# Holding back the second expert's gathers and the weight sums, and making queries and keys for four sequences at a time, in a two-layer transformer kernel

## The chip, the cores and the metric

The kernel runs on one core of a Trainium2 chip. The metric is the device time of one execution in microseconds (us), lower is better. Several executions of the kernel before are shown by their median; one further execution was recorded by the hardware profiler, and every view below comes from that one. All data is float32 except for a few small one-hot products.

## The reference

The input x has 32 sequences of 128 tokens of 512 numbers. Two layers follow one another.

```python
# layer 0
h   = layernorm(x) + silu(cond) @ W_ada.T
q, k, v = 16 heads of 64 of h @ Wqkv.T;  q, k normed per head
x   = x + softmax(q k.T / 8) v @ Wout.T
tok = x.reshape(4096, 512)
gate = softmax(tok @ Wgate.T)                 # 8 experts
vals, idx = top_k(gate.T, 512)                # each expert picks 512 tokens
g   = layernorm(tok[idx])
y   = gelu_tanh(g @ fc1[e].T) @ fc2[e].T * vals
tok = tok.at[idx].add(y)
# layer 1
n   = adaln1(x, cond);  q, k, v = n @ wq.T + bq, n @ wk.T + bk, n @ wv.T + bv   # 16 heads of 32
x   = x + softmax(q k.T / sqrt(32)) v @ wo.T + bo
x   = x + gelu(adaln2(x, cond) @ w1.T + b1) @ w2.T + b2
```

## The kernel before

**The schedule.** All work is written as operations handed to a scheduler of the kernel's own (`Sched.op`): the engine or engines that may do it, an estimated duration, what it reads (`r`) and writes (`w`), and a priority. When the kernel is built, `Sched.run` plays a clock over these and fixes one order of instructions for each engine; buffers of SBUF and banks of PSUM are given out in that order too. On the chip each engine follows its order and waits by semaphores. So a change of a dependence or of a priority constant can move many instructions. A buffer made with `stands` is no memory; it only orders operations.

**Products.** Most matrix products are cut into blocks of two by two and made with seven block products instead of eight (Strassen in Winograd's form). This needs sums of blocks: of the operands ahead (VectorE, line L1310, or GpSimd, L1311) and of the results behind. Results gather in three PSUM banks, named X, Y and Z, of which one is read (copied by ScalarE or added by VectorE) between two products into it.

**Weight sums.** The last layer's two MLP matrices are cut twice, so that they need sums of blocks of blocks. These are made once, in 22 steps (`w1_outer`, `w2_outer`, `w1_inner`, `w2_inner`) in the shade of layer 0 and of the experts. A step loads four blocks by one `fetch` (L2549, tiles `w1r`, `w2r`, SyncE's queue), adds them on VectorE or GpSimd (tiles `w1n`, `w2n`), and stores the sums by `put` (L2554).

**From layer 0 to the experts.** The last projections of layer 0 (L1976, added at L1984) are stored as tokens (L1991, `tok` and `acc`). For each of 8 experts four indirect DMAs, issued by GpSimd (L2208), gather 128 chosen tokens each into `xg`. VectorE takes their statistics (L501, L502, L504), two small ScalarE activations and three small VectorE operations make the inverse root (L465 to L473), and L2272 writes the normed tile `xng`. TensorE transposes it (L1283, tile `tpg`), ScalarE or VectorE evicts the transposes into `gT` (L2284, L2282), and the products with the first expert matrix begin (L2322), followed by those with the second (L2386). For expert 0 these are spread: the first two tiles are normed one by one, the other two together. While TensorE has nothing to do it runs a few idle products (`spun`, L1225) and finds the tokens of expert 1 (L2143 to L2170). A copy named `fence` (L2214) waits for the fourth gather of expert 0, and later loads wait behind it. The gathers of expert 1 have priority `pe_ - 1000`, ahead of nearly all else.

**The last layer.** The 32 sequences are 16 groups of two (`group(g)`); two groups make one four (`G`, 8 in all), for which the MLP is made at once (`up`, L3027, then `down`, L3109). A group norms its sequences into `nT`, makes queries and keys by `prod_qk` (L2755): in each of seven products q and k stand side by side in one bank, and each matmul has 128 columns of one block row of the group as its moving operand. Values and the output projection come from `chain_T` (L2799) with 256 moving columns of weights. Then come scores (L2855), exponentials (L2859), sums and weighted values (L2867, L2873), the output projection and the second norm. The MLP products of the four before fill TensorE while a group's norms and exponentials are made. MLP weights stream in as pieces of 256 KB, of which `STREAM` may be under way; `gate = inner_done[-(n):][:1]` lets a chain of seven products begin only when the n-th last one is nearly done.

Of the kernel before, what the change touches and what calls it, by code (L numbers as in the profile page):

```python
# [13 lines left out]
AF = mybir.ActivationFunctionType  # L14
# [5 lines left out]
P = 128  # L20
# [1173 lines left out]
def fast_kernel(ctx: ExitStack, tc: tile.TileContext, x, condT, mask, cols, w_ada, wqkv, wout, wout_p, wout_o, wgate,  # L1194
# [998 lines left out]
    def expert(e, after):  # L2193
# [13 lines left out]
        for h in range(NH):  # L2207
            sch.op(POOL, 1.2, lambda h=h: nc.gpsimd.indirect_dma_start(  # L2208
                out=xg[h].t, out_offset=None, in_=tok[:, :],
                in_offset=bass.IndirectOffsetOnAxis(ap=idx[:, e, h : h + 1], axis=0)),  # L2210
                w=[xg[h]], r=[tok_b, (idx_b, e)], lat=2.5, prio=pe_ - 1000 if e == 1 else pe_, job=job)
# [55 lines left out]
        for h in range(NH):  # L2267
            if e == 0 and h == 2:
                norm0((2, 3), pe_ - 1, [xn])
            xn, tp = row(f"xng_{e}_{h}"), bank(f"tpg_{e}_{h}")  # L2270
            mv, y, z = stat[h]
            sch.op(DVE, dve_us(D, 2, True), lambda xn=xn, h=h, mv=mv, y=y, z=z: nc.vector.tensor_scalar(  # L2272
                xn.t, xg[h].t[:, :D], mv.t[:, 2 * z : 2 * z + 1], y.t[:, z : z + 1], ALU.subtract, ALU.mult),
                w=[xn], r=[xg[h], mv, y], prio=px[h], job=job)
# [267 lines left out]

    step_done, room_for, first_steps = [], [(17)], (10)

    def fetch(pieces, pr, job):
# [4 lines left out]
        sch.op(SP, 0.24, f_, w=[b_ for b_, _, _ in pieces], r=[x for _, _, r in pieces for x in r] + step_done[-(2):][:1], lat=4.0, prio=pr,  # L2550
# [64 lines left out]
    for n, step in enumerate(steps):  # L2615
        g = 3 + (3 + n) // 2 - 1
        step_done.append(stands(None))
        if n == first_steps:
            room_for.append((13))
        if n < first_steps:  # L2620
# [3 lines left out]

    for m, (n, s_) in enumerate(at_w):
# [94 lines left out]
    def group(g):  # L2720
        b0 = g * GB
        G, sub = divmod(g, 2)
        pr = LB + G * 1000.0
        pr -= {0: (87), 1: (112), NG4 - 1: (54)}.get(G, 100) - 100
        pn, pat, job = pr - (806) + (12) * sub, pr + (100) + (34) * sub, LJ + G
# [8 lines left out]
        else:  # L2734
            for i in range(GB):
                norm_T([x2[i]], nT, ss1, ss1_b, b0, f"a1_{g}_{i}", pn + i, job, i, True)
                seen_v.append((st.v, 4 + i, 1))


        pp = pn + 8  # L2740
# [49 lines left out]
        def chain_T(n, Bn, rB, Tv, Tn, pr, once, after):  # L2790

            X, Y, Z = (bank(f"{n}{c}_{g}", (P, QD)) for c in "xyz")

            def prod(b_, what, lhs, rr, fresh=True, keep=0):
                w_, wb = l1w[n + what]

                def f_():
                    for k in range(2):
                        nc.tensor.matmul(b_.t, lhs()[:, k, :], w_()[:, k, :], start=fresh and k == 0, stop=True, skip_group_check=True)  # L2799
                sch.op(PE, mm_us(QD, 2), f_, w=[b_], r=rr + [wb], prio=pr, job=job, keep=keep)  # L2800

            prod(X, "11", lambda: Bn(1, 1), [*rB(1, 1), Y, Z], keep=KEEP_A)
            prod(Z, "s1", lambda: Tv(1), [Tn[1]])
            once(1, X)
            prod(Y, "12", lambda: Bn(2, 1), rB(2, 1))
            once(5, Z)
            prod(X, "s2", lambda: Tv(2), [Tn[2]], False)
            after(1, 1, Y)
            once(2, X)
            prod(Z, "s4", lambda: Bn(2, 2), rB(2, 2), False)  # L2810
            prod(X, "s3", lambda: Tv(3), [Tn[3]], False)
            after(1, 2, Z)
            once(3, X)
            prod(X, "22", lambda: Tv(4), [Tn[4]], False)
            after(2, 1, X)

# [18 lines left out]
        chain_T("v", N_, rN, NTv, NTn, pp + 1, once_v, after_v)  # L2835


        x3 = x2
        oTs, both = [], []
        for i in range(GB):  # L2840
# [9 lines left out]
            def quads(scs=scs, i=i):  # L2850
                for t in range(4):
                    for r in range(4):
                        rs = slice(r * 32, r * 32 + 32)
                        qk_ = qk[1 + t // 2, 1 + i].t
                        nc.tensor.matmul(scs[r].t[:, t, :], qk_[rs, 1, t % 2, :], qk_[rs, 0, t % 2, :], start=t == 0, stop=True,  # L2855
                                         skip_group_check=True)
            sch.op(PE, mm_us(S, 5), quads, w=scs, r=[qk[1, 1 + i], qk[2, 1 + i]] + ([gelus[G - 1]] if G else []), prio=pa + 1, job=job)
# [11 lines left out]
            def outs(po=po, pe=pe, i=i):  # L2869
                for t in range(4):  # L2870
                    for r in range(4):
                        h = 4 * t + r
                        nc.tensor.matmul(po.t[r * 32 : r * 32 + 32, t, :], v[i].t[:, h * HD1 : (h + 1) * HD1],  # L2873
# [415 lines left out]
```

## Time and profile before

| | us |
|---|---|
| median of 3 runs | 3107.63 |
| the runs | 3107.51, 3114.08, 3107.63 |
| the profiled execution, its own time | 3113.92 |
| span of its records | 3112.2 |
| TensorE busy | 3074.4 |
| VectorE busy | 2256.6 |
| GpSimd busy | 1284.7 |
| ScalarE busy | 1267.4 |

The span runs from the first to the last record; the profiled execution's own time holds a little more. Windows are given in us from the start of the span: layer 0 lasts to about 1042, the experts to about 1846, the last layer to the end. In a line of the timeline the columns are start and length in us, engine, line of the kernel, operation, output and inputs, shapes and count, and in square brackets the idle time of the engine just before, with what ended it. PE is TensorE, PEld its weight loads, DVE VectorE, ACT ScalarE, POOL GpSimd, SP SyncE. A matmul of float32 leaves two records. The clock is TensorE's granted clock as a share of the full one.

### The profile page before, as it was taken

What the parts mean: (1) busy time and instruction counts of PE and PEld (TensorE: products, weight loads), DVE (VectorE), ACT (ScalarE), POOL (GpSimd) and SP (SyncE); (2) the same over time, 40 slices, a digit from 0 to 9 for tenths busy, and PEclk for the clock granted to TensorE, in tenths of its full rate; (3) what the DMA queues carried; (4) which work ended last, traced back from release to release, by engine and by line L of the source; (5) the groups of instructions that cost most, each with busy time, mean ns of one, the idle gap of its engine ahead of it and who ended that gap; (6) DMA issues with size and microseconds to landing.
All of it is one profiled execution on the core that took longest, in us unless ns stands there. A gap on an engine that the chain in (4) does not pass through costs nothing. (4 is left out here: it accounts for less than half of the span.)

```text
span 3112.2 us, 60678 instructions
## 1 busy us (share of the span) xinstructions
PE 3074.4 (99%) x22656; PEld 2514.9 (81%) x22656; DVE 2256.6 (73%) x4490; ACT 1267.4 (41%) x3241; POOL 1284.7 (41%) x1030
## 2 busy tenths in 40 slices
PE   9999999999999999999999999999999999999998
PEld 5655555555588788888888888999999999999997
DVE  8877888889866688666665446786767676767675
ACT  4455565556500222221222114545463636364543
POOL 2412524434220367765666510334343424243525
PEclk9999999999999999999999999999999999999999
DMA  7556757756585865443333361655555556566576
GB/s 278 190 199 232 240 188 245 265 195 203 186 275 195 278 210 183 112 112 104 111 104 109 99 183 48 197 181 180 187 180 181 184 176 190 170 191 193 170 228 201
DMA packets 350672, 571.97 MB, mean 184 GB/s; under 512 B 33258, under 2 KB 114722, under 8 KB 350114
## 3 DMA queue, kind: packets, MB, share of 16 engines
q1 hardware_dynamic: 341714, 550.38, 54.1%
q0 software_dynamic: 7168, 16.91, 2.8%
q8 instruction: 182, 2.98, 0.4%
q14 instruction: 120, 0.98, 0.1%
q10 hardware_dynamic: 1488, 0.71, 0.1%
HBM read 473.62 MB, written 94.27 MB: 182 GB/s over the span
## 5 line engine op out<-in xcount | busy, mean ns | idle before, releaser
L1311 POOL TENSOR_TENSOR base<-base,base 128x512 f32<-128x512 f32 x335 | 450.6, 1359 | 789.4 <-DVE base L3078 445.9
L3109 PE MATMUL bank<-base,base 128*128 128x128 f32 x3048 | 365.1, 278 | 6.6 <-POOL base L1311 3.5
L3109 PEld LDWEIGHTS bank<-base,base 128*128 128x128 f32 x3048 | 354.2, 193 | 13.8 <-POOL base L1311 3.9
L3027 PE MATMUL bank<-base,base 128*128 128x128 f32 x3048 | 361.6, 275 | 0.5 <-ACT bank L2989 0.2
L3027 PEld LDWEIGHTS bank<-base,base 128*128 128x128 f32 x3048 | 354.3, 192 | 4.6 <-ACT bank L2989 1.2
L1310 DVE TENSOR_TENSOR base<-base,base 128x512 f32<-128x512 f32 (+2 forms) x476 | 307.5, 666 | 35.7 <-ACT base L2971 12.7
L2333 ACT ACTIVATE h<-h,prm 128x256 f32<-128x256 f32 x256 | 114.9, 502 | 255.5 <-DVE h L2327 240.6
L2386 PE MATMUL d<-fc,h 128*128 128x256 f32 x992 | 218.9, 379 | 0.0
L2386 PEld LDWEIGHTS d<-fc,h 128*128 128x128 f32 x992 | 188.0, 190 | 25.3
L3037 ACT ACTIVATE base<-base,prm 128x128 f32<-128x128 f32 x512 | 169.2, 397 | 49.7 <-DVE base L3072 29.2
L2322 PE MATMUL u<-gT,fc 128*128 128x256 f32 x768 | 179.1, 383 | 0.9 <-ACT gT L2284 0.9
L2322 PEld LDWEIGHTS u<-gT,fc 128*128 128x128 f32 x768 | 147.4, 192 | 21.6 <-ACT gT L2284 1.3
L2327 DVE TENSOR_TENSOR h<-v,u 128x512 f32<-128x512 f32 x128 | 86.2, 682 | 65.5 <-PE u L2322 59.5
L2322 PE MATMUL u<-tg,s 128*128 128x256 f32 x512 | 120.9, 379 | 0.0
L2386 PE MATMUL d<-t,hs 128*128 128x256 f32 x512 | 113.4, 379 | 0.0
L2418 POOL DMA_INDIRECT acc<-y,idx x32 | 50.7, 1584 | 149.3 <-DVE y L2411 79.2
L3072 DVE TENSOR_TENSOR base<-bank,base 128x512 f32<-128x512 f32 x96 | 66.0, 688 | 59.5 <-PE bank L3027 54.6
L2322 PEld LDWEIGHTS u<-tg,s 128*128 128x128 f32 x512 | 97.3, 190 | 13.2
L2386 PEld LDWEIGHTS d<-t,hs 128*128 128x128 f32 x512 | 97.2, 190 | 13.2
L3078 DVE TENSOR_TENSOR base<-bank,base 128x512 f32<-128x512 f32 x120 | 82.0, 688 | 30.1 <-PE bank L3027 15.2
L2859 ACT ACTIVATE base<-bank,mbT 128x512 f32<-128x512 f32 x128 | 81.9, 687 | 45.6 <-PE bank L2855 31.5
L2799 PE MATMUL bank<-base,base 128*128 128x256 f32 x384 | 98.1, 382 | 1.3 <-DVE base L2894 0.4
(1880 smaller groups left out, 6858.6 us busy)
## 6 DMA issues: line engine op xcount, KB each, us to landing
base<-w1i SPq DMA_DIRECT2D x224, 256.0 KB
base<-w2i SPq DMA_DIRECT2D x224, 256.0 KB
base<-w2s SPq DMA_DIRECT2D x168, 256.0 KB
fc<-in_fc_dram SPq DMA_DIRECT2D x64, 512.0 KB
fc<-in_fc_dram SPq DMA_DIRECT2D x32, 1024.0 KB
base<-w1s SPq DMA_DIRECT2D x96, 256.0 KB
base<-in_w_dram SPq DMA_DIRECT2D x72, 256.0 KB
otd<-oT SPq DMA_DIRECT2D x56, 256.0 KB
```

Of the source, the lines that this page charges most:

```text
L1310: ways = {DVE: (DVE, dve_us(n), lambda: nc.vector.tensor_tensor(o_(), a_(), b_(), op_)), POOL: (POOL, 0.2 + n / 480, lambda: nc.gpsimd.ten ...
L1311: POOL: (POOL, 0.2 + n / 480, lambda: nc.gpsimd.tensor_tensor(o_(), a_(), b_(), op_))}
L2322: nc.tensor.matmul(ps[n].t[:, t, :], lhs()[:, k, t * P : (t + 1) * P], rhs.t[:, k, :], start=(k == 0), stop=(k == 1))
L2327: sch.op(DVE, dve_us(D), lambda: nc.vector.tensor_tensor(o_.t, a_.t, ps[n].t, ALU.add), w=[o_], r=[a_, ps[n]], prio=pr, job=job)
L2333: sch.op(ACT, act_us(HQ, 1), lambda t=t, c=c: nc.scalar.activation(o_.t[:, t, :], o_.t[:, t, :], AF.Gelu_apprx_tanh, bias=col("b1s", e * 1 ...
L2386: nc.tensor.matmul(ps[n].t[:, j, :], lhs[m].t[:, k, t * P : (t + 1) * P], rhs.t[:, 2 * m + k, :], start=(m == 0 and k == 0), stop=(m == NM ...
L2799: nc.tensor.matmul(b_.t, lhs()[:, k, :], w_()[:, k, :], start=fresh and k == 0, stop=True, skip_group_check=True)
L2859: sch.op(ACT, act_us(D, 1), lambda sc=scs[r], pe=pe[r], b=b: nc.scalar.activation(pe.t, sc.t, AF.Exp, bias=mbT[:, b : b + 1], scale=sm1), ...
L3027: nc.tensor.matmul(b_.t[:, u, :], w_.t[:, u * P : (u + 1) * P], x_(), start=fresh and u == 0, stop=True, skip_group_check=True)
L3037: sch.op(ACT, act_us(S, 1), lambda k=k, u=u, c=c: nc.scalar.activation(o_[k].t[:, u * S : (u + 1) * S], o_[k].t[:, u * S : (u + 1) * S], A ...
L3078: sch.op(DVE, dve_us(D), lambda: nc.vector.tensor_tensor(d_[k].t, flat(src), flat(t_), ALU.add), w=[d_[k]], r=[src, t_], prio=po - 3000, j ...
L3109: nc.tensor.matmul(b_.t, x_()[:, k * S : (k + 1) * S], w_.t[:, k, :], start=fresh and k == 0, stop=True, skip_group_check=True)
```

## The change

Three things change, with a set of constants.

1. The norms of expert 0 write a marker, `ends["normed"]`. The gathers of expert 1 read it, and so do the loads (`fetch`) of the weight-sum steps from number 13 on (`after_norm`). Both are therefore ordered behind all four norms of expert 0.
2. `group` is split into `places`, `norms`, `pair_products` (the old form), `quad_products` and `attend`. The first four keeps the old form for its two groups. For the seven others `quad_products` makes queries and keys of four sequences at once: q and k are two chains of seven products with a bank set each, the moving operand has 256 columns (both sequences of a group), and the two block columns are the two groups. Values are made by `chain_T` with twice as many columns of the bank for the same weights.
3. Constants: priorities in `places`, `up` and `down`, `STREAM` 14 to 13, the gates of `chained` (11 to 0, and `[-0:][:1]` is the first chain of all) and `seeded` (20 to 40).

```diff
-                w=[xg[h]], r=[tok_b, (idx_b, e)], lat=2.5, prio=pe_ - 1000 if e == 1 else pe_, job=job)
+                w=[xg[h]], r=[tok_b, (idx_b, e), *(ends["normed"] if e == 1 else [])], lat=2.5, prio=pe_ - 1000 if e == 1 else pe_, job=job)
...
+            normed = [] if e else [stands(None)]
+            if e == 0:
+                ends["normed"] = normed
...
-                w=[xn], r=[xg[h], mv, y], prio=px[h], job=job)
+                w=[xn, *normed], r=[xg[h], mv, y], prio=px[h], job=job)
...
+    after_norm = [[]]
...
-        sch.op(SP, 0.24, f_, w=[b_ for b_, _, _ in pieces], r=[x for _, _, r in pieces for x in r] + step_done[-(2):][:1], lat=4.0, prio=pr,
+        sch.op(SP, 0.24, f_, w=[b_ for b_, _, _ in pieces], r=[x for _, _, r in pieces for x in r] + step_done[-(2):][:1] + after_norm[-1], lat=4.0, prio=pr,
...
+        if n == 12:
+            after_norm.append(ends["normed"])
...
-        pr -= {0: (87), 1: (112), NG4 - 1: (54)}.get(G, 100) - 100
+        pr -= {0: (90), 1: (112), NG4 - 1: (54)}.get(G, 100) - 100
...
+    def chain_T(n, g, job, Bn, rB, Tv, Tn, pr, once, after, two=False):
+        X, Y, Z = (bank(f"{n}{c}_{g}", (P, 2, QD) if two else (P, QD)) for c in "xyz")
...
+                for m in range(2 if two else 1):
+                    for k in range(2):
+                        nc.tensor.matmul(b_.t[:, m, :] if two else b_.t, lhs()[:, k, m * S : (m + 1) * S], w_()[:, k, :],
+                                         start=fresh and m == k == 0, stop=True, skip_group_check=True)
...
+    def quad_products(G, nTs):
+        pp, job = places(2 * G + 1)[1] + 8, LJ + G
+        N_ = lambda j, l: nTs[l - 1][j - 1].t
...
+        Tn = {n: row(f"n1f{n}_{G}", (P, 2, GT)) for n in (1, 2, 3, 4)}
+        for n, a_, b_ in ((1, nTs[1][0], nTs[0][0]), (2, nTs[1][1], Tn[1]), (3, nTs[1][1], nTs[1][0]), (4, nTs[0][1], Tn[2])):
+            tt(lambda n=n: Tn[n].t, lambda a_=a_: a_.t, lambda b_=b_: b_.t, ALU.subtract, D, [Tn[n]], [a_, b_], pp, job, DVE, False)
+        qk = {}
+        for z in "qk":
...
+            X, Z, Y = (bank(f"{z}{c}_{G}", (P, 2, GT), c == "y") for c in "xzy")
+            t_ = row(f"{z}t_{G}", (P, 2, GT))
...
+                    for u in range(2):
+                        for k in range(2):
+                            nc.tensor.matmul(b_.t[:, u, :], w_()[:, k, u * P : (u + 1) * P], rhs()[:, k, :],
+                                             start=fresh and u == k == 0, stop=True, skip_group_check=True)
...
+            prod(X, "11", lambda: N_(1, 1), rN(1, 1), True, KEEP_A, [Y, Z])
+            prod(Z, "s1", lambda: Tn[1].t, [Tn[1]], True)
+            biased(Y, X, 1, pp - 2)
+            prod(X, "s2", lambda: Tn[2].t, [Tn[2]], False)
+            copied(t_, Z, pp - 1)
+            prod(Y, "12", lambda: N_(2, 1), rN(2, 1), False)
+            biased(Z, X, 1, pp - 2)
+            prod(X, "s3", lambda: Tn[3].t, [Tn[3]], False)
...
+        chain_T("v", f"q{G}", job, N_, rN, lambda n: Tn[n].t, {n: Tn[n] for n in Tn}, pp + 1, once_v, after_v, True)
...
-            pa = pat + (13) * i
+            pa = pat + (16) * i
...
-    STREAM = (14)
+    STREAM = (13)
...
-        gate = inner_done[-(11):][:1]
+        gate = inner_done[-(0):][:1]
...
-        gate = inner_done[-(20):][:1]
+        gate = inner_done[-(40):][:1]
...
-        pr, job = LB + G * 1000.0 + 200 - ({0: (132), NG4 - 2: (135), NG4 - 1: (300)}.get(G, 100) - 100), LJ + G
+        pr, job = LB + G * 1000.0 + 200 - ({0: (132), NG4 - 2: (138), NG4 - 1: (600)}.get(G, 100) - 100), LJ + G
...
-        pr, job = LB + G * 1000.0 + (1137) - ({0: (91), NG4 - 2: (2), NG4 - 1: (1241)}.get(G, 100) - 100), LJ + G
+        pr, job = LB + G * 1000.0 + (1154) - ({0: (0), NG4 - 2: (2), NG4 - 1: (1491)}.get(G, 100) - 100), LJ + G
...
-        form(s1_, a21, a22, ALU.add, pr - (470))
+        form(s1_, a21, a22, ALU.add, pr - (420))
...
-        form(a21, a11, a21, ALU.subtract, pr - (987))
+        form(a21, a11, a21, ALU.subtract, pr - (1037))
...
     for G in range(NG4):
-        got = [group(2 * G + z) for z in range(2)]
+        on = [norms(2 * G + z) for z in range(2)]
+        if G:
+            how = quad_products(G, [nT for _, nT in on])
+        else:
+            how = [pair_products(z, on[z][1]) for z in range(2)]
+        got = [attend(2 * G + z, *on[z], *how[z]) for z in range(2)]
```

## The prediction

> **What bounds the kernel.** I read the share of each engine first, then the windows with the granted clock, then the timeline at the places where TensorE is not full, and the waits of TensorE last.
>
> ```profile
> PE 3074.4 (99%) x22656; PEld 2514.9 (81%) x22656; DVE 2256.6 (73%) x4490; ACT 1267.4 (41%) x3241; POOL 1284.7 (41%) x1030
> ```
>
> TensorE is busy for 3074.4 of 3112.2 us. Only two things can shorten the kernel by much: less TensorE work, or a removed piece of its 38 us of idle time. The windows say where that idle time lies: 7.3 us in 1012:1089 (layer 0 ends, the experts begin), 14.1 us in 2957:3112 (the tail), 3.0 us in 1859:1945 (entry of the last layer), and only 2.7 us in the 1012 us of 1945:2957, the steady part of the last layer. Start of the experts, in 2 us windows (TensorE busy, granted clock, DMA share, GB/s):
>
> ```profile
> 1040.00:1042.00 2.00, 2.00 (x21) 1.00 1.06 416
> 1042.00:1044.00 2.00, 0.74 (x7) 1.00 1.05 413
> 1044.00:1046.00 2.00, 0.00 (x0) 1.00 0.95 327
> 1046.00:1048.00 2.00, 0.00 (x0) 0.67 0.82 248
> ...
> 1054.00:1056.00 2.00, 2.00 (x6) 0.50 1.00 317
> 1056.00:1058.00 2.00, 2.00 (x12) 0.77 1.05 402
> ```
>
> TensorE stops for six microseconds while the DMA engines are full, the clock falls to half at about 1046.7 and comes back at about 1056.9. The timeline of all engines over the same stretch names the chain:
>
> ```profile
> 1035.52 1.46 POOL L2208 DMA_INDIRECT xg<-tok,idx  x1 [3.49 <-DMA acc<-xl]
> ...
> 1042.83 0.69 DVE L501 BATCH_NORM_STATS2 ng_0st<-xg 128x6 f32<-128x512 f32 x1 [0.79 <-DMA xg<-tok,idx]
> ...
> 1046.44 2.15 DVE L2272 TENSOR_SCALAR xng<-xg,ng_0mv,ng_0y 128x512 f32<-128x512 f32 x1
> ...
> 1048.65 2.16 PE L1283 MATMUL tpg<-ident,xng 128*128 128x128 f32 x8 [5.91 <-DVE xng L2272]
> ...
> 1051.71 5.41 PE L2322 MATMUL u<-gT,fc 128*128 128x256 f32 x12 [0.90 <-ACT gT L2284]
> ```
>
> Gather, statistics, norm, transpose, first product. Two links are long for a reason that the change touches. The gather takes 7.31 us from its issue to its statistics; of a later expert, with an empty hardware queue, the same takes 3.93 us (the second one of expert 0: 7.77 against 3.98):
>
> ```profile
> 1508.88 1.28 POOL L2208 DMA_INDIRECT xg<-tok,idx  x1
> ...
> 1512.81 0.68 DVE L501 BATCH_NORM_STATS2 ng_6st<-xg 128x6 f32<-128x512 f32 x1
> ```
>
> And the norm (xng) takes 2.15 us where each later one takes 0.54 to 0.55, while GpSimd issues a gather of expert 1 and then adds weights (L1311). The DMA view by single microseconds shows what the gather stands behind: in 1039:1040 the SyncE queue alone is full, and the gathers' queue (q0) appears only at 1041.
>
> ```profile
> q1 hardware_dynamic: 223, 0.41, 105.4%
> ```
>
> **Part 1, the start of the experts.** The order of the changed program shows what leaves the window 1022 to 1048. Gone from ahead of the fence copy on SyncE are eight loads of w1r (2 MB, issued at 1022.3 and 1034.45) and two stores of sums (0.5 MB, 1036.35); the four gathers of expert 1 (1042.3 to 1047.0, 0.95 us each on GpSimd) and one GpSimd sum go behind the fourth norm; four VectorE sums of 0.68 to 0.69 us leave the stretch between the last projection and the second pair of norms. The start of the first gather (1035.52) stays: it waits for token stores, which are not moved. With 3.95 us it would have its statistics at 1039.5, and the second at 1041.2. VectorE then works in its new order: statistics, aggregate, variance; the two index operations of expert 1, which began at 1041.68 after a wait for TensorE and which I leave there (to 1042.04); second statistics 0.7; three small operations 0.6; two more 0.4; norm 0.55, done at 1044.3. ScalarE's two small activations (0.62) and three small operations (0.6) give the second norm at 1045.6. Its transposes end at 1046.2; ScalarE needs 1.45 us for the first tile's evictions (2.90 for two tiles at 1049.80) and 0.73 for half of the second's, so the first product starts at 1047.25 instead of 1051.71: **4.5 us**. If the index operations need not wait so long it is 6; if the gathers gain only half (the acc and bias copies of 0.75 MB still stand before them), 2.5. Who waits for the added waits: expert 1's gathers sit at the head of GpSimd's queue until the fourth norm, with nothing behind them that the first products need (their weight sums were made before); expert 1's statistics are first needed for norms near 1129, so some 40 us cover them. The weight sums of steps 13 to 22 sink into the experts, where VectorE is busy 101 and GpSimd 107 of 155 us, and the last of them still lies at the start of expert 2, of eight: priced at nothing; without that cover each would cost what it lasts, 0.68 us.
>
> The clock: products at half speed from 1051.71 to 1056.9 lost 2.6 us. After the change TensorE still pauses 1.7 us and then 1.05 us with two transposes between. The rows go both ways: a pause of 2.72 us before 397.21 was followed by 3.4 us at half clock (0.57 in 398:402), one of 2.1 us in 480:490 was not (1.00). I credit half, 1.3 us, with ends 0 and 2.6. The Trainium skill speaks against the credit: "TensorE: Matmul & The Clock Gate", Part 4, says that transposes do not count as TensorE activity in the same way, and Part 1 that one idle window of about 3.4 us halves the clock; by that the pause would be 4.5 us long and the clock could fall as before, so the credit would be 0. No run here separates it.
>
> **Part 2, queries and keys for four sequences.** The order shows that groups 0 and 1 keep the old form, and the other 14 groups become 7 fours. The rows:
>
> ```profile
> 2145.37 1.06 PE L2755 MATMUL bank<-base,wq 128*128 128x128 f32 x8
> 2146.26 1.06 PE L2755 MATMUL bank<-base,wk 128*128 128x128 f32 x8
> ...
> 2100.03 1.03 PE L2799 MATMUL bank<-wv,base 128*128 128x256 f32 x4
> 2100.90 1.03 PE L2799 MATMUL bank<-base,base 128*128 128x256 f32 x4
> ```
>
> Eight records with 128 moving columns step every 0.89 us, 0.1115 each; four with 256 every 0.865 us, 0.216 each. L2755 has 1792 records, 112 per group. Before, 14 groups: 1568 x 0.1115 = 174.8 us. After: 784 x 0.2163 = 169.5 us. That is **5.3 us** less, and since TensorE is full there it is on the path. Bounds: 0 if columns cost as much as before, 5.5 at the expert rows' rate (16 records in 3.45 us). The values' products keep their count; their evictions and the operand differences become fewer and wider (per four, eight VectorE subtractions of 256 columns at 0.49 us become four of 512 at 0.69), off the path, since VectorE is busy 72% of the steady part.
>
> What it adds: q and k become two chains of seven with 1.73 us per product, each evicted by two ScalarE operations (by the 0.50 us of 128x256 rows, 1.0 us) and a handover of 0.2 to 0.3. Another product of 1.73 us in between hides that, and the new order has one almost everywhere. I take 0.5 us in all, with ends 0 and 3.5 (0.5 per four). At the entry the old form gave the first attention some 37 us of products of groups 2 and 3 as filler; the new order puts only four q and one z products there, and the last six output products of group 1 come nearly one after the other; such dependent steps cost 0.84 and 0.38 us at 1925 and 1927. I take 1 us, ends 0 and 4.
>
> **Part 3, priorities, gates, 13 pieces of the weight stream.** In the steady part 2.7 us can be gained at most. In the tail TensorE waits 0.56, 0.85, 0.18 and 3.35 us for VectorE and GpSimd, then runs 6.8 us at half clock (3.4 us lost). The new order has 17 products instead of 16 between the last first-matrix product and the first that needs the late sums, which is 0.9 us more cover, but moves four late additions from VectorE to GpSimd. I take 0, ends -5 and +4.
>
> **Sum.** Against the profiled execution's 3113.92 us: -4.5 -1.3 -5.3 +0.5 +1.0 = -9.6, so 3104.3. The median of the runs shown is 3107.63, two runs at 3107.5 and one at 3114.1. The two half-clock stretches cost 2.6 + 3.4 = 6.0 us in the profiled execution, about the 6.3 by which it stands above the median; I take it, as an estimate, that the faster runs lack them. From the median the clock credit falls away: 3107.6 - 8.3 = **3099**.
>
> **Rivals.** (a) The four-wide chains stall TensorE: a bank is now evicted whole and its next product waits. Price 1.3 us for each eviction without filler; 8.3/7 = 1.2 us per four is the point from which it decides, that is one bare eviction in each four; two make 7 x 2.6 = 18.2, three 27, with the other gains kept 3117 and more. For it: 12 such handovers per four. Against it: 2.7 us of idle time in 1012 us with the same kind of handover, and fillers seen in the order. Time 3110 to 3120. (b) The gather is late for GpSimd's and its queue's own reasons, not for the loads: then Part 1 gives only the 1.6 us of the norm, and 3107.6 - 1.6 - 5.3 + 1.5 = 3102 to 3104, no change or nearly. (c) The tail loses its luck: up to +4, 3103, again near no change; with a longer clock stretch 3106.
>
> **How the numbers follow.** About 0.2% (6.2 us) is what a measurement of this kernel can tell from no change: faster is below 3101.4, slower above 3113.8. My forecast has 0.65, of which 0.62 lies below that bound; (b) and (c) together 0.2, of which 0.08 is below it; (a) 0.15. So faster 0.70, same 0.15, slower 0.15. The forecast's own ends: -6 -2.6 -5.5 and the tail's -5 would be 3088, but not all at once; I set 3090. At the top I go to 3111, into (a), and leave some 0.2 outside.
>
> **What would show it.** Right: the wait for xng below 2.5 us, the first statistics near 1039.5, the norm at 0.55 us; q and k products 0.865 us per four records of 256 columns, TensorE idle in the steady part at most 5 us; last-layer start to end 5 us shorter. Wrong: first statistics still at 1042 with an empty q1 (b); waits of L2755's successor for ScalarE of more than 1 us per four (a).

## The result, and the profile after

The changed kernel takes 3120.27 us (median of 11 runs, 3118.92 to 3123.33), the kernel before 3112.66 us (11 runs, 3107.51 to 3115.41): a ratio of 1.0028, with a 95% interval from 1.0019 to 1.0038. It is slower: by 0.24% between the medians, by 0.28% by that ratio of the runs. The forecast was 3099, its range ended at 3111. The profiled execution of the changed kernel took 3119.58 us with a span of 3117.8.

The share of each engine, the changed kernel:

```profile
PE 3072.8 (99%) x21872; PEld 2490.1 (80%) x21872; DVE 2269.8 (73%) x4418; ACT 1261.6 (40%) x3161; POOL 1278.6 (41%) x1029
```

TensorE has 784 records fewer, as worked out. It is busy 1.6 us less (3074.4 before) in a span that is 5.6 us longer, so idle time has grown. The windows of the changed kernel say where (TensorE busy, its weight loads, VectorE, ScalarE, GpSimd, granted clock, DMA share, GB/s):

```profile
1012.00:1089.00 77.00, 74.20 (x442) 65.42 (x441) 50.80 (x109) 20.24 (x47) 35.00 (x31) 0.98 0.74 250
1089.00:1200.00 111.00, 104.87 (x482) 91.70 (x481) 98.17 (x137) 22.52 (x51) 58.37 (x43) 0.97 0.52 161
1200.00:1300.00 100.00, 96.31 (x475) 84.44 (x474) 75.24 (x113) 19.94 (x45) 65.27 (x50) 0.98 0.63 197
1300.00:1400.00 100.00, 99.31 (x495) 87.10 (x494) 73.38 (x113) 23.40 (x53) 58.43 (x43) 1.00 0.41 117
```

In 1012:1089 TensorE is idle 2.8 us, where it was 7.3: the start of the experts gained what it should. But 1089:1400, where TensorE was never idle before, now has 10.5 us of idle time, and the clock falls twice. Those are, above all, the passes of experts 1 and 2, where the prediction set a price of nothing.

The start of the experts, timeline of the changed kernel (first gather, its statistics, first norm, first product):

```profile
1035.91 1.36 POOL L2208 DMA_INDIRECT xg<-tok,idx  x1 [14.45 <-DMA acc<-xl]
...
1039.72 0.70 DVE L501 BATCH_NORM_STATS2 ng_0st<-xg 128x6 f32<-128x512 f32 x1 [1.48 <-DMA xg<-tok,idx]
...
1043.60 0.54 DVE L2275 TENSOR_SCALAR xng<-xg,ng_0mv,ng_0y 128x512 f32<-128x512 f32 x1
...
1046.79 4.26 PE L2325 MATMUL u<-gT,fc 128*128 128x256 f32 x12 [0.77 <-ACT gT L2287]
```

The gather now takes 3.81 us to its statistics, the norm 0.54 us. The lost time, in expert 1 (timeline of all engines, the changed kernel):

```profile
1165.17 1.82 POOL L2421 DMA_INDIRECT acc<-y,idx  x1 [0.77 <-DVE hs L1310]
...
1166.07 17.39 DVE L1310 TENSOR_TENSOR h<-h,h 128x512 f32<-128x512 f32 x1
...
1166.45 1.84 POOL L1311 TENSOR_TENSOR hs<-hs,h 128x512 f32<-128x512 f32 x1
...
1167.68 5.49 POOL L1311 TENSOR_TENSOR t<-fc,fc 128x512 f32<-128x512 f32 x4
...
1172.59 5.46 POOL L1311 TENSOR_TENSOR t<-fc,t 128x512 f32<-128x512 f32 x4
...
1177.48 5.42 POOL L1311 TENSOR_TENSOR fc<-fc,fc 128x512 f32<-128x512 f32 x4
...
1183.38 1.47 DVE L2330 TENSOR_TENSOR v<-v,u 128x512 f32<-128x512 f32 x2
...
1184.16 3.75 PE L2325 MATMUL u<-gT,fc 128*128 128x256 f32 x8 [6.13 <-issue]
```

One VectorE operation that takes 0.68 us elsewhere lasts 17.39 us. It forms the difference of two hidden blocks, both in SBUF (a form, below, is such a sum or difference, tiles `h` and `hs`). All that time GpSimd runs 13 operations in one piece: a form, then the twelve weight differences of the expert (t, t, fc). Behind the held operation VectorE's queue stands still, and in it the additions that empty the PSUM banks (v<-v,u); TensorE runs on for 12 us, to 1178.03, then stops for 6.13 us and goes on when the first of these additions is done (that it stopped for want of a bank is read from this order; no row says it). The held operation begins while GpSimd still issues the scatter (L2421), and ends 0.56 us after the last difference. In expert 2 the same operation lasts 15.52 us, and TensorE stops for 3.69. The page names "issue" or VectorE as the releaser; the cause stands on GpSimd's rows.

Split at fixed places (the last projection's end; expert 0's first product; its first product of the second matrix; the first TensorE work behind expert 7; the last layer's first transposes), in us:

| profile | last projection to first product | expert 0, first matrix | experts to the end | last layer |
|---|---|---|---|---|
| before | 19.80 | 52.77 | 741.98 | 1252.5 |
| changed | 14.58 | 51.62 | 758.03 | 1248.3 |
| difference | -5.22 | -1.15 | +16.05 | -4.2 |

With +0.3 ahead of the first place and -0.1 between the last two, this is the 5.6 us of the spans. Of the 16.05, 10.5 are the idle time; TensorE at half clock after each stop (1182.8 to 1189.6 and 1295.4 to 1298.9 by the granted clock) loses some 4.4 more, and 1.1 I can't place.

Queries and keys, as foreseen, take 1.72 us for 8 records of 256 columns (0.215 each), and TensorE passes from them to another product without a gap:

```profile
1925.75 1.89 PE L2878 MATMUL bank<-base,wq 128*128 128x256 f32 x8
1927.47 1.89 PE L2760 MATMUL bank<-wo,base 128*128 128x256 f32 x8
```

### The profile page after: what moved, and what is told of

It is laid out like the page before. It is cut to its first block, busy times and chain, and to the rows that moved or that the text cites. A ratio compares the mean times of both kernels' runs of the same rounds, so it can differ in the third digit from the quotient of the medians.

```text
span 3117.8 us, 58938 instructions
## 1 busy us (share of the span) xinstructions
PE 3072.8 (99%) x21872; PEld 2490.1 (80%) x21872; DVE 2269.8 (73%) x4418; ACT 1261.6 (40%) x3161; POOL 1278.6 (41%) x1029
## 4 chain that ended last, share of the span: by engine, by line
PE 54%; DVE 1%; POOL 1%; DMA 1%; issue 1%; ACT 0%; DVEq 0%; POOLq 0%; SPq 0%; ACTq 0%
PE bank L3141 10%; PE bank L3223 10%; PE d L2389 9%; PE u L2325 8%; PE bank L2760 6%; PE bank L2878 5%; PE bank L2967 1%; PE bank L2979 1%; PE bank L2987 1%; PE bank L1283 1%; PE bank L2797 1%; POOL base L1311 1%; DVE base L1310 0%; DMA acc<-y,idx 0%; PE tpg L1283 0%
## 5 line engine op out<-in xcount | busy, mean ns | idle before, releaser
L3223 PE MATMUL bank<-base,base 128*128 128x128 f32 x3040 | 364.7, 277 | 6.8 <-POOL base L1311 5.3
L3223 PEld LDWEIGHTS bank<-base,base 128*128 128x128 f32 x3040 | 353.4, 193 | 14.6 <-POOL base L1311 7.3
L1310 DVE TENSOR_TENSOR base<-base,base 128x512 f32<-128x512 f32 (+2 forms) x456 | 296.0, 672 | 36.7 <-ACT base L3085 13.0
L2421 POOL DMA_INDIRECT acc<-y,idx x32 | 50.6, 1581 | 146.3 <-DVE y L2414 66.5
L1475 ACT ACTIVATE sq<-qk 128x512 f32<-128x512 f32 x128 | 78.4, 631 | 50.7 <-DVE qk L1525 18.8
```

What stands on the lines that cost most here:

```text
L1310: ways = {DVE: (DVE, dve_us(n), lambda: nc.vector.tensor_tensor(o_(), a_(), b_(), op_)), POOL: (POOL, 0.2 + n / 480, lambda: nc.gpsimd.ten ...
L3223: nc.tensor.matmul(b_.t, x_()[:, k * S : (k + 1) * S], w_.t[:, k, :], start=fresh and k == 0, stop=True, skip_group_check=True)
```

## The experiments

Theory A: the held VectorE operation is the cause; it can't start while GpSimd runs without a pause. Theory B: the weight sums, moved into the experts, are too much work there. Theory C: their transfers are in the way of the experts' weights. "Before" is the kernel before, timed in the same series as the run.

| run | median us | before | ratio, 95% interval |
|---|---|---|---|
| e1, no sums' wait | 3104.83 | 3113.19 | 0.9975 (0.9965 to 0.9985) |
| e2, no gathers' wait | 3114.84 | 3113.19 | 1.0005 (0.9995 to 1.0015) |
| e4, forms on GpSimd | 3105.26 | 3113.19 | 0.9975 (0.9965 to 0.9985) |
| e6, rests | 3100.65 | 3113.19 | 0.9964 (0.9950 to 0.9978) |
| e7, changed kernel again | 3117.82 | 3111.53 | 1.0021 (1.0012 to 1.0031) |
| e11, one more, two SBUF inputs | 3111.18 | 3111.53 | 1.0000 (0.9990 to 1.0009) |
| e12, one more, one SBUF input | 3111.21 | 3111.53 | 1.0001 (0.9991 to 1.0011) |
| e3, neither wait | 3106.79 | 3111.53 | 0.9989 (0.9979 to 0.9999) |
| e14, e11 behind the scatter | 3115.13 | 3112.18 | 1.0007 (0.9997 to 1.0016) |
| e15, e12 behind the scatter | 3114.16 | 3112.18 | 1.0006 (0.9996 to 1.0015) |
| e9, fours, old constants | 3125.27 | 3112.18 | 1.0042 (1.0027 to 1.0056) |
| e10, rests, no gathers' wait | 3104.59 | 3112.18 | 0.9978 (0.9968 to 0.9987) |
| e16, forms behind the run | 3127.35 | 3111.96 | 1.0050 (1.0033 to 1.0066) |
| e17, all forms behind the run | 3124.14 | 3111.96 | 1.0043 (1.0029 to 1.0058) |

**Which of the two waits (e1, e2).**

```
e1:  -        if n == 12: after_norm.append(ends["normed"])
e2:  -        r=[..., *(ends["normed"] if e == 1 else [])]   # of the gathers
```

> The changed kernel with one wait undone: the weight sums of steps 13 to 22 no longer wait for the first expert's norms; expert 1's gathers still do, and the rest of the change stays. All theories lay the loss of the changed kernel to 1089:1400, where TensorE stood still for 6.13 and 3.69 us and ran at half clock after both. Theory A (a blocked VectorE operation): with the sums back in their old places GpSimd's twelve weight differences of experts 1 and 2 are again broken up by operations that wait for VectorE, no VectorE operation stays over 6 us, and TensorE is idle under 1 us in 1089:1400. The last layer keeps its 4.2 us. The start of the experts keeps what the gathers' wait alone gives, 1.6 us (the norm at 0.55 us) to 6.1 (all of it). Against the kernel before (3112.7): 3102 to 3107. Theory B (the sums are simply too much work inside the experts) and theory C (their transfers take the time of the expert weights) expect the same here. If instead the gathers' wait made the loss, this run stays at 3118 to 3121.

> The changed kernel with the other wait undone: expert 1's gathers go as early as before, the weight sums still wait. Theories A, B and C all expect the stops of 1089:1400 to stay (idle 8 to 12 us there), and the start of the experts to lose up to 2.2 us of its gain (the norm back at 2.15 us): 3118 to 3123. Theory A expects one VectorE operation of 12 to 18 us with two SBUF inputs in expert 1 and one in expert 2, each over a run of twelve or more GpSimd operations. If the gathers' wait made the loss, 3104 to 3108.

In e1 "experts to the end" is 741.98 us, to the hundredth that of the kernel before; no VectorE operation of experts 1 and 2 lasts over 4 us. In e2 it is 758.84, with held operations of 17.36 and 16.02 us. So the sums' wait alone makes the loss. It also makes the gain at the start: first product 13.59 us after the last projection in e2, 18.50 in e1. For the gathers' wait that is 1.3 us alone, in one profile, and nothing on top of the other; the 1.3 are not clear of chance, since the nine profiles with neither wait have 18.13 to 20.19 us, and the norm lasts 0.54 us in four of them too (e9, e12, e16, e17). e2's run time of 3114.84 lies below its expectation though its experts are as slow as expected.

**The held operation itself (e4, e6).**

```
e4:  forms h, hs:  tt(..., pr + 15 + n, job, *((POOL, False) if e in (1, 2) else ()))
e6:  + if e in (1, 2) and m in (1, 2):
     +     sch.op(POOL, 0.2, lambda: nc.gpsimd.tensor_tensor(rest, v[:, 0, :1], v[:, 1, :1], ALU.add),
     +            w=[rest], r=[v], prio=pe_ + 399.5 + m, ...)
```

> The changed kernel, with all waits, but in experts 1 and 2 the sums and differences of the hidden blocks (h, hs: two SBUF inputs) run on GpSimd only, none on VectorE. Theory A (such an operation stood on VectorE for 17.39 and 15.52 us while GpSimd ran 13 operations without a pause; the PSUM additions queued behind it, the banks stayed full, TensorE stopped): the stops vanish, TensorE idle under 2 us in 1089:1400, and the 16.1 us that the stage grew come back: 3104, between 3102 and 3108. Theory B (too much work for the two engines): GpSimd gets still more (24 operations of 1.27 us in two experts), so the wait moves to another place: 3114 to 3124. Theory C (transfers): nothing changes, 3118 to 3122.

> The changed kernel, and in experts 1 and 2 two tiny GpSimd additions (one element wide) more each, which read a block that VectorE has just made, so that GpSimd has to wait for VectorE after the first four and after some eight of its twelve weight differences. Work is only added. Theory A: the blocked VectorE operation gets in at the pause, so it lasts 6 us at most (5.4 us is what it takes behind four such differences in experts 3 to 7 of both kernels, where TensorE does not stop); TensorE idle under 2 us in 1089:1400; 3103 to 3107. Theory B: more work, same or longer, 3118 to 3124. Theory C: 3118 to 3122.

e4: both stops are gone, but "experts to the end" is still 749.43, for GpSimd now delivers the forms late. The waits of TensorE in e4, 1012:1400 (us in all, times, longest):

```profile
PE d L2390 <- POOL hs L1311: 4.0, 2, 3.3
```

e6 adds work and is the fastest kernel here, 0.36% below the kernel before and so faster than both. Its timeline in expert 1:

```profile
1162.93 7.65 DVE L1310 TENSOR_TENSOR h<-h,h 128x512 f32<-128x512 f32 x1
...
1164.55 5.47 POOL L1311 TENSOR_TENSOR t<-fc,fc 128x512 f32<-128x512 f32 x4
...
1172.05 0.19 POOL L2355 TENSOR_TENSOR rest<-v 128x1 f32<-128x1 f32 x1 [2.03 <-DVE v L2330]
...
1172.20 4.98 POOL L1311 TENSOR_TENSOR t<-fc,t 128x512 f32<-128x512 f32 x4
```

GpSimd waits 2.03 us for VectorE in the middle of its differences, and the held operation ends there, after 7.65 us; TensorE is idle 1.8 us in 1089:1400. The sums and their transfers still wait for the norms and the last sum ends nearly as late (1270 us, 1276 in the changed kernel), though the scheduler has moved a few sums between the two engines; GpSimd is busy longer than in the changed kernel (208.5 us of 1089:1400 against 182.1). So B and C fall. A pause of GpSimd is what was missing. The sizes were off: 6 us at most was expected for the held operation, and 3103 to 3107 for the kernel.

**The changed kernel again, and without both waits (e7, e3).**

> The changed kernel as it is, timed beside the next three so that all share the same runs of the kernel before. Theory A (a VectorE operation with two SBUF inputs stays out for as long as GpSimd runs without a pause): 3115 to 3121, with the two long operations at 15 to 18 us and TensorE idle 9 to 11 us in 1089:1400 again. If those were an accident of one execution, 3103 to 3106.

> The changed kernel with both new waits undone: the queries and keys for four sequences and the new constants alone. From the profiles so far the last layer is 4.2 us shorter in the changed kernel and 5.6 to 7.1 us in the four experiments (the prediction had 3.8), and the start of the experts is as before (first product some 19.8 us after the last projection). So 3105.5 to 3109, with TensorE idle under 1 us in 1089:1400. If the four-wide products gave nothing and the experiments' gains came from elsewhere, 3112 to 3114.

e7 repeats: operations of 17.37 and 15.60 us, stops of 5.8 and 3.8, 758.07 us. e3 is the last layer alone: 1245.9 us of it against 1252.5, and 741.97 in the experts.

**One operation more (e11, e12, e14, e15).** If a long run of GpSimd is all it takes, one added operation must do it in the kernel before.

```
e11, e12:  differences of expert 1:  pe_ - 600 + (0 if e == 1 else 1000) + n
e11:  + v3 = max(v3, v3)   (VectorE, expert 1, m == 1)      e12:  + v3 = v2 + u7
e14, e15:  e11, e12, and the forms of expert 1, m == 0, on GpSimd
```

> The kernel before, with its own sums, gathers and last layer. In expert 1 the twelve weight differences of GpSimd are put ahead of the weight sums, so that they run in one piece (about 15 us), and VectorE does one added operation of 0.68 us just after they begin: v3 = max(v3, v3), two SBUF inputs. Theory A: that one operation lasts 12 to 16 us, TensorE stops for 4 to 7 us in expert 1 and then runs at half clock for some 3 us more: 7 to 10 us over the kernel before, 3119 to 3123. Theory B (too much work, or late weights): 0.7 us of VectorE's work is not felt: 3111 to 3115.

> The same kernel with the same place and almost the same time of VectorE's work, but the added operation has one SBUF input and one PSUM input: v3 = v2 + u7 is made a second time. In both kernels the additions of this form keep their 0.68 us while GpSimd runs. Theory A: it lasts 0.7 us, no stop, 3111 to 3115, as the kernel before. If any added operation at this place, or the new order of GpSimd's differences, made the loss, it is as slow as the one with two SBUF inputs, 3119 to 3123.

A miss for theory A. In e11 the twelve differences run in one piece, and yet (timeline):

```profile
1173.65 5.47 POOL L1311 TENSOR_TENSOR t<-fc,fc 128x512 f32<-128x512 f32 x4
...
1174.47 1.04 DVE L2347 TENSOR_TENSOR v<-v 128x512 f32<-128x512 f32 x1
```

It waits for the one GpSimd operation that is running, and gets in. So I compared GpSimd's rows one by one. In the changed kernel each of the 13 lasts 1.8 us, but the next begins 1.23 us after it: they overlap. The rows above show it, where four last 5.49 us and the next four begin 4.91 us after their start. In e11 (and behind e6's rest) most last 1.27 us, and the next begins as one ends (at most 0.06 us before): they do not overlap. The overlap begins with the first operation behind a scatter's issue (L2421, which it overlaps by half a microsecond), as do all 142 overlapping runs in the 16 traces, and goes on until GpSimd has waited for something. The kernel before has it too, in experts 3 to 7, for four operations, after which GpSimd waits for VectorE:

```profile
1365.56 1.55 POOL L2418 DMA_INDIRECT acc<-y,idx  x1 [4.13 <-DMA acc<-y,idx]
1366.57 5.51 POOL L1311 TENSOR_TENSOR t<-fc,fc 128x512 f32<-128x512 f32 x4
1367.19 5.45 DVE L1310 TENSOR_TENSOR hs<-h,h 128x512 f32<-128x512 f32 x1 [0.98 <-ACT h L2333]
```

In expert 1 of the kernel before the overlap ends after one operation, and not at a weight sum (timeline):

```profile
1171.98 2.72 DVE L1310 TENSOR_TENSOR h<-h,h 128x512 f32<-128x512 f32 x1
...
1172.32 1.82 POOL L1311 TENSOR_TENSOR hs<-hs,h 128x512 f32<-128x512 f32 x1
...
1174.22 1.61 POOL L1311 TENSOR_TENSOR hs<-h,hs 128x512 f32<-128x512 f32 x1
...
1175.80 5.04 POOL L1311 TENSOR_TENSOR t<-fc,fc 128x512 f32<-128x512 f32 x4
```

The second form on GpSimd reads what the first has just written, and begins 0.08 us after its end. From there the differences, two sums among them, follow one another without overlap and without a pause. In the changed kernel the scheduler gave this second form to VectorE (at 1194.58), and the differences stand directly behind the first. The traces divide by this: with the form on GpSimd one addition overlaps in expert 1 (before, e1, e3, e9, e11, e12, e16, e17), with the form on VectorE 13 (the changed kernel, e2, e7). So what broke the run in e1 was not a wait for VectorE, as had been expected. No run moves this one form by itself.

The rule that comes of it, that a form of two SBUF inputs stays out while GpSimd's operations overlap, is theory A2. e14 was meant to carry the overlap into e11's run:

> The run with the one added VectorE operation of two SBUF inputs, with one thing more: in expert 1 the four forms of the first hidden block run on GpSimd, so that from the last scatter (acc<-y) on GpSimd never waits for VectorE and its operations follow one another into the twelve weight differences. Before this, that added operation took 1.04 us, against theory A. Theory A2, made from the traces since: GpSimd operations behind a scatter's issue overlap (each lasts 1.8 us, the next begins 1.23 us later), and a VectorE operation with two SBUF inputs gets in only where they do not overlap, that is after GpSimd has paused; in the ten traces so far every one of these that took over 4 us began on overlapping GpSimd operations. A2: the added operation lasts 10 to 15 us, TensorE stops for 1 to 4 us in expert 1 and its clock falls: 3 to 8 us over the kernel before, 3114 to 3120. If the length of the run or the kind of operation decide and not the overlap, it takes 1 to 2 us as in the run before, 3109 to 3113.

> Its twin: the added operation has one SBUF and one PSUM input, all else is the same, GpSimd's overlapping run too. A2: 0.7 us, no stop, 3109 to 3113, the kernel before. If the new order of GpSimd's work itself costs time, as slow as its twin.

A miss again, and one that decides nothing: in e14 the second form had to wait for the first one on GpSimd itself, the overlap ended there (1.27 us each from then on), and the added operation took 0.88 us. TensorE did not stop in either. That e14's time lies in A2's range is luck: its twin, expected at 3109 to 3113, took 3114.16, and neither is clear of the kernel before.

**Long overlap without added work (e16, e17).** In the kernel before the overlapping four are followed by a wait of GpSimd. e16 takes it away.

```
forms of experts 3 to 7, m == 0:   e16: last three, e17: all four on GpSimd,
   r=[a_, b_, (Bf[1, 2], 3)]   (behind the last weight difference)
```

> The kernel before, no work added. In experts 3 to 7 the last three forms of the first hidden block go on GpSimd behind its twelve weight differences, so that from the last scatter on GpSimd no longer waits for VectorE after the first four of them (that wait ends VectorE's 5.4 us on the first form in the kernel before). The first form, two SBUF inputs, stays on VectorE. Theory A2 (such an operation stays out while GpSimd operations overlap behind a scatter's issue): it lasts 13 to 17 us instead of 5.4 in each of the five experts, TensorE stops for 3 to 6 us and runs at half clock after it: 6 to 9 us for each, 3140 to 3158. If long operations are not made by this (overlap ends by itself, or another wait breaks it), 5 to 6 us and 3109 to 3115.

> Its control: the first form too goes on GpSimd behind the differences, so that no VectorE operation with two SBUF inputs stands beside the overlapping run; the run itself is the same. A2: no long operation, no stop, 3108 to 3116. If the late forms or GpSimd's order make the loss of the first kernel, as slow as that one.

e16, timeline of expert 3:

```profile
1362.73 5.51 POOL L1311 TENSOR_TENSOR t<-fc,fc 128x512 f32<-128x512 f32 x4
...
1363.78 14.76 DVE L1310 TENSOR_TENSOR hs<-h,h 128x512 f32<-128x512 f32 x1 [0.97 <-ACT h L2333]
...
1378.62 1.27 POOL L1311 TENSOR_TENSOR hs<-hs,h 128x512 f32<-128x512 f32 x1 [0.64 <-DVE hs L1310]
```

In all five experts the first form lasts 14.5 to 16.3 us, where it was 5.0 to 5.5. A2 holds in its durations. Its price was too high: the stops are 0.4 to 3.2 us long, the experts grow by 17.5 us and not by 30 to 45. The control e17 is not the clean control I meant, and took 3124.14 where 3108 to 3116 was expected. In experts 3 and 4 another VectorE operation with two SBUF inputs, the one-hot table of the routing (bf16), falls into the run; in experts 5 to 7 none does:

```profile
1364.84 18.05 DVE L2143 TENSOR_TENSOR oh<-iota_jb,lo 128x1024 bf16<-128x1024 bf16 x1
...
1575.39 5.50 POOL L1311 TENSOR_TENSOR t<-fc,fc 128x512 f32<-128x512 f32 x4
...
1577.92 0.69 DVE L2327 TENSOR_TENSOR h<-v,u 128x512 f32<-128x512 f32 x1 [2.83 <-PE u L2322]
```

Experts 3 and 4 lose 6.9 and 4.6 us, experts 5 to 7 nothing (from expert 5's first product on, all stages as long as before), with the same overlapping run and the same late forms. That is the control, inside one kernel. The last row shows why the PSUM additions alone do no harm: one SBUF and one PSUM input, 0.69 us beside overlapping operations.

Counted over the 16 traces, for the VectorE operations of L1310 (sums and differences of SBUF blocks) that begin while a GpSimd addition or subtraction runs, with overlap where the next GpSimd operation begins over 0.25 us before that one ends: 4467 began on one without overlap, 3 of them lasted over 2 us, the longest 3.78; 72 began on one with overlap, and all 72 lasted over 2 us. Every one that lasted over 4 us ended 0.56 us after the last operation of the overlapping run (1.09 us for the bf16 table). The held operation does not make the overlap: in experts 5 to 7 of e17 13 additions overlap with none beside them. The PSUM additions v<-v,u and h<-v,u: 2254, none over 0.69 us, overlap or not. The Trainium skill, "SBUF — State Buffer", section "Who interferes with whom", says that a VectorE instruction with two SBUF inputs and a GpSimd instruction that reads SBUF block each other, and one with at most one SBUF input, outside its two-port modes, does not. The traces agree on both. By that page the loser waits for the one instruction that came first; here it waited for 13 (17.39 us against 1.8 for the longest of them), and the measurement decides.

**The last layer's constants (e9).**

```
e3 with places {0: 87}, pa = pat + 13*i, STREAM 14, gates -11 and -20, down 1137 {0: 91, 7: 1241}, ...
```

> The queries and keys for four sequences alone: both waits undone and all priorities, gates and the stream's length as in the kernel before. With the new constants the same (both waits undone) took 3106.8 against 3111.5, its last layer 6.6 us shorter than that of the kernel before in the profile. By the prediction the four-wide products are worth 3.8 us net and the constants nothing: 3105 to 3109. If the constants carry the gain, 3110 to 3114, and the last layer as long as before.

A plain miss. The fours with the old constants are slower than before: a last layer of 1264.1 us, 11.6 over the kernel before and 18.2 over e3. Waits of TensorE in 1945:2957 of e9 (11.9 us in all, 1.7 before and 1.2 after):

```profile
PE bank L3223 <- issue: 6.6, 5, 1.3
PE bank L3223 <- POOL base L1311: 2.4, 6, 0.5
```

They lie at the products of the second matrix (L3223), not at the queries and keys. That accounts for some 11 of the 18. Two stretches at half clock in the same part (at 2189.7 and 2657.3, 3.41 us each; none there in e3) lose up to 3.4 more, and the rest I can't place. No run has the new constants with the old form of queries and keys, so what each of the two is worth by itself is not shown.

**The version that the runs point to (e10).** e6 without the gathers' wait.

> The version that the runs point to: the changed kernel with the two tiny waiting GpSimd additions in experts 1 and 2, and without the gathers' wait. In the profiles the first product came 13.6 us after the last projection with the sums' wait alone and 13.5 to 14.6 with both, so that the gathers' wait adds nothing. A2: no VectorE operation over 8 us in experts 1 and 2, TensorE idle under 2 us in 1089:1400, 3098 to 3103, as with the gathers' wait (3100.7). If the gathers' wait is worth its 1.6 us (the norm), 3102 to 3105.

Faster than before, but with 3104.59 outside the 3098 to 3103 of A2 and not better than e6 (3100.65, in another series). No operation over 8 us, as expected; TensorE waits 2.0 us for VectorE once more. The time fits the other branch, that the gathers' wait is worth something; but 4.1 us of it are in the last layer (3.1 us shorter than before, 7.2 in e6), where the gathers have no part, so that stays open. e6 remains the best.

## Why the prediction was wrong

**The step that failed** is one sentence of Part 1: the weight sums "sink into the experts, where VectorE is busy 101 and GpSimd 107 of 155 us ... priced at nothing; without that cover each would cost what it lasts, 0.68 us". Measured: 16.05 us, 9.1 in expert 1 and 7.0 in expert 2, which turns a sum of -9.6 into a loss. The share of busy time was the wrong measure, and it was read beside the place: 101 and 107 us are those of 1245:1400, while the moved sums run from 1061 to 1276 (the last of them ended at 1213 before); in 1089:1244 the kernel before has VectorE busy 130.8 and GpSimd 104.4 of 155 us. Yet the amount of work is not the cause, as e6 shows. With the sums moved, the scheduler gave VectorE a form of expert 1 whose wait of 0.08 us on GpSimd had ended the overlap behind the scatter, and in expert 2 another form (h<-h,h, on GpSimd before). What was left is a run of 13 to 16 overlapping additions, and beside it a two-input form; in expert 1 that form had its place there before too, and lasted 2.72 us. The order of the changed program shows who does which form, and I had read it for queues and not for what runs beside what. The profile of before had the sign: first forms of 5.0 to 5.5 us in experts 3 to 7, which cost nothing there and which I did not follow up, though I had read a like effect for the norm (2.15 us beside GpSimd against 0.54). Of the 21.3 us between the forecast and the measured time this step is 16.05; 5.0 are the base, below.

**What was right, with its sizes.** The gather stood behind the loads: statistics forecast at 1039.5, seen at 1039.72; first product forecast at 1047.25, seen at 1046.79 (-5.22 from the last projection's end, forecast -4.5). Rival (b), the gather late for its own queue, falls with e1, where the loads stay and the gather takes 7.37 us to its statistics, against 3.79 in e2, where they wait. The clock credit, forecast 1.3, came out as 1.15, and 0.9 to 2.4 in the experiments with the early start; its size is not sharp, for expert 0's first matrix takes 50.38 to 51.90 us in the six profiles with the early start and 51.68 to 53.04 in the ten others. What the prediction drew from the Trainium skill ("TensorE: Matmul & The Clock Gate", Parts 1 and 4), that the clock could fall as before and the credit be 0, did not come: half clock at this start lasted 3.41 us in the changed kernel, e2, e7 and e10 and did not occur in e4 and e6, where the ten others have 6.83 or 10.24. The last layer was forecast at -3.8 and came to -4.2, to -6.1 in e7, and from -3.1 to -7.2 in the experiments with the new constants.

**Right by luck.** The last layer's -3.8 was the sum of a Part 2 that gains and a Part 3 at 0. By e9 the constants are worth 18.2 us beside the fours, and without them the fours lose, so that the sum fits is luck. Rival (a) is refuted for this kernel (waits of 1.2 us in the steady part); the fours with the old constants do lose, but at the second matrix (L3223) and not where (a) looked.

**The base.** I took 3107.6 for the median and argued that the faster runs lack the half-clock stretches. The later series put the kernel before at 3111.5 to 3113.2, near the profiled 3113.92; three runs were too few, and the argument does not hold. From the profiled execution the sum was 3104.3. That e1, which undoes the failed step, measures 3104.83 is luck too: it has little of the start's gain (18.50 us to the first product, 14.58 in the changed kernel), and its last layer is 6.2 us shorter instead of 3.8. Whole spans can't tell such terms apart: layer 0, which no run changes, ends between 1028.31 and 1033.74 us in the 16 profiles.

## What to carry to other kernels

Before work is moved off an engine's queue, ask what the waits there were good for, and which other operations change engines with it: here a wait of 0.08 us on GpSimd was the gap that let VectorE's operations with two SBUF inputs in, and without it every PSUM addition queued behind the held one had to wait too. In a profile, look for VectorE rows far above their usual time and read GpSimd's rows beside them; where a row's duration exceeds the distance to the next, the operations overlap. A change of tile width and the priorities that were set for the old width are one change: try them apart before saying which of them gains.

## What the runs showed of the hardware

A VectorE operation of L1310 with two SBUF inputs that began on a GpSimd addition without overlap lasted under 2 us in all but 3 of 4467 cases (3.78 at the most); beside overlapping ones it was held until 0.56 us after the end of the run: 5.4 us for four, 17.39 for 13, and 18.05 for a bf16 table. A GpSimd addition of one element that had to wait for VectorE ended the overlap (e6), and so did one that waited 0.08 us for GpSimd's own last result (expert 1 of the kernel before). Why operations behind a scatter's issue overlap was not tried. The granted clock is held in steps: of the 78 half-clock stretches in the traces 62 last 3.41, 6.83 or 10.24 us, one, two or three times 3.41; the other 16 are the last of each trace and run past its last record. So the early start of the experts cost a step of 3.41 us in four profiles and none in two (e4, e6), with expert 0's first matrix 1.2 to 1.5 us apart.
